# A fixed order on VectorE at the end of each recurrent step: r·h of the third batch's halves placed ahead of the first pair's last update and turns

## The chip, the cores and the metric

The kernel runs on one core of a Trainium2 chip. Its engines, with the names that the profile uses, are TensorE (PE, with PEld for the loading of its weights), VectorE (DVE), ScalarE (ACT), GpSimd (POOL) and SyncE (SP), whose queue issues nearly all of the transfers. The metric is the device time of one execution in microseconds; lower is better.

## The reference, cut to what matters

Two layers over 16 graphs of 1024 nodes with 128 features each, all with one 1024×1024 matrix `adj`. Layer 0 is one graph convolution; layer 1 is a gated recurrent cell, run five times, that aggregates over the graph in every step. Both end in a residual sum and a layernorm.

```python
support = einsum('bnf,fo->bno', x, weight)                       # layer 0
x = layernorm(x + einsum('nm,bmo->bno', adj, support) + bias)

def step(h):                                                     # layer 1, five times
    m  = einsum('nm,bmd->bnd', adj, h)                           # m_in and m_out: the same matrix
    av = concatenate([m, m], axis=-1)
    u3 = h @ u3_w.T + u3_b
    z  = sigmoid(av @ w3_w.T + w3_b + u3)
    r  = sigmoid(av @ w4_w.T + w4_b + u3)
    hv = tanh(av @ w5_w.T + w5_b + (r * h @ u5_w.T + u5_b))
    return (1 - z) * h + z * hv
x = layernorm(x + h_after_five_steps)
```

All is float32. One step for a graph is thus: aggregate, two gates z and r, the product r·h, the candidate hv, and the update h + z·(hv − h).

## The kernel before

The 16 graphs are worked in four quads of four; a graph of a quad is called a batch here and has a number k from 0 to 3. Layer 0 runs over the quads once. Layer 1 is `for q in range(NQ): for s in range(STEPS)`, 20 steps, and the change lies in this loop. A step's tensors for a quad stay on the chip: `rows` holds h with the nodes on the partitions, for the aggregation; `hid` holds h with the features on the partitions, for the gates and the update; `agg` holds the aggregated rows.

**A step has three parts.** First `aggregate` multiplies by `adj` with a seven-product scheme for 2×2 blocks, used on two levels. The outer level's seven products come as four chains, named by their numbers 12, 3, 67 and 54. Each chain (function `chain`, matmuls on L427) makes seven inner products in the order 1, 5, 6, 2, 7, 3, 4, of 1.73 us each where two outer products are made side by side. Inner product 1 of chain 12 reads `rows` of batch 0. Products 5, 6, 7 and 4 read sums that VectorE makes in `inner_sums` (L346 to L349, here called S1 to S4): S1 is a difference of batch 1 and batch 0, S2 is made from S1, and products 5 and 6 wait for them.

Secondly, `gates_of_pair` makes the gates of batches 0 and 1 together, again by seven products (L666, L685 to L691), and `reset_products` (L715) finishes the candidate's matmuls. `update` then does each half of each batch: a tanh on ScalarE (L723) and three instructions on VectorE, subtract (L724), multiply (L725), add into `hid` (L726), each working on the result of the one before. `turn_rows` (L737) transposes a whole batch of `hid` into the buffer `ypad`, and its two transfers (L748, 256 KB each) write it to the DRAM buffer `turned`; `fetch_rows` (L757, four transfers of 128 KB for a batch) reads `turned` back into `rows`, for the next step. Each of the two turns writes a part of both batches' buffers, so the fetch of batch 0 needs both turns. The last step of a quad (`last`) does otherwise: it turns to `closing` and reads the next quad's state into `hid`, while the next quad's rows come by `load_pairs` and `load` (L810, L113) right after the aggregation.

Thirdly come batches 2 and 3, in half batches called units 4 to 7. For each unit there are `gate_first` (L540, u3 product, and its copy L548), `gate_r` (L558, sigmoid L561, then r·h on VectorE, L568), `gate_z` (L573, L576), `update_products` (L581 with w5, then L582 with u5, which needs r·h), and in `update_half` a tanh (L592) and again three instructions on VectorE (L597, L598, L599). Behind unit 5 batch 2 is turned, and behind each of units 6 and 7 half of batch 3, with their fetches. S1 to S4 of the next step are made between the updates of units 6 and 7:

```python
        if urgent and h == 1:
            next_sums[0] = first_sums(rows)
            pinned(next(next_sums[0]))
```

**What sets the order.** TensorE's matmuls here, the transfers, and some instructions of VectorE are given to `tc.keep_in_program_order` (`in_order`, and `put` where it is passed); such instructions of an engine keep the order in which they are written. The rest may be moved by the framework's scheduler when the program is built; semaphores keep the data right in any case. `pin` pins only while `strict` is set, which here it is not. In a step that isn't the last of its quad, VectorE's built order from the first update is, with T for a turn of a batch, ru for r·h of unit u, and s, m, a for the three instructions of an update (the digits after them: batch, half for the first pair; unit for the rest):

```
s(0,0) m s(1,0) a m s(0,1) a m s(1,1) a m  T0  a  r4  T1  s4 m4 r5 a4 s5 m5 r6 a5  T2  r7  S1  s6 m6 a6 T3a S2 s7 m7 a7 T3b S3 S4
```

In the last step of a quad the next quad's sums (S1 to S4 of rows 0 and 1, and four smaller ones of rows 2 and 3) aren't pinned, and the scheduler has put them among the instructions of the gates of the first pair and ahead of the first update: one ahead of L657, two between it and L688, five after it.

ScalarE's and TensorE's order around this: L540 of units 4 and 5, L558 and L573 of unit 4, L540 of unit 6, L581 and L582 of unit 4, L558, L573 of unit 5, L540 of unit 7, L581, L582 of unit 5, L558 and L573 of unit 6, of unit 7, L581 and L582 of unit 6, of unit 7, then inner product 1 of the next step. In the last step of a quad the four matmuls of inner product 1 stand between L581 and L582 of unit 4.

## Time and profile before

| what | value |
|---|---|
| time, median of 3 runs | 1887.28 us (1886.15 to 1887.92) |
| the profiled execution's own time | 1888.17 us |
| its span, first to last instruction | 1886.0 us |
| TensorE busy | 1816.3 us, 96% of the span, 7092 matmuls |
| VectorE busy | 1404.3 us, 74% |
| ScalarE busy | 804.9 us, 43% |
| transfers | 161.42 MB, 86 GB/s over the span; 405328 of 421306 packets under 512 B |
| granted TensorE clock, mean | 0.980 |

In this profile a busy share is no distance from a limit: TensorE is busy for 96%, and that includes stretches at half clock. What a stage waits for is read from the table of waits (engine, line, and the engine and line that released it: total us, times, longest us), from the timeline (start, duration, engine, line, tile written and tiles read, count, and in brackets the idle time before the first of them and its releaser), and from the table of stretches (busy time of each engine in a stretch, then the granted TensorE clock, the transfer engines' busy share and GB/s). The profiled execution's own time is 2.2 us above its span and 0.9 us above the median of the runs.

### The profile page before, as it was taken

The page shows a single profiled execution, that of the slowest core. Times are in us where ns is not written, and L with a number is a line of the kernel's source. Part 1 is how long each engine was busy: PE and PEld are TensorE (multiplying, and loading weights), DVE is VectorE, ACT ScalarE, POOL GpSimd, SP SyncE. Part 2 cuts the span into 40 slices and gives each one's busy share as a digit, 9 for nine tenths or more (in the row PEclk, how much of TensorE's full clock was granted, in tenths as well). Part 3 has the DMA queues.
Part 4 walks back from the last instruction along what each step waited for, and adds up shares of the span by engine and source line. Part 5 has one row for each costly group of instructions (what it writes and reads, how often), then busy time and mean ns, then how long its engine had stood idle before and what let it go on. Part 6 is the DMA issues. An engine that isn't in the chain of part 4 may idle for free.

```text
span 1886.0 us, 21009 instructions
## 1 busy us (share of the span) xinstructions
PE 1816.3 (96%) x7092; PEld 1280.5 (68%) x7092; DVE 1404.3 (74%) x2492; ACT 804.9 (43%) x1464; POOL 102.0 (5%) x152
## 2 busy tenths in 40 slices
PE   8999999999999999999999999999999999999998
PEld 7888876674857667585765748576674757667484
DVE  6977777776686857777777767777776577777668
ACT  3355554434242443435343442534444352543436
POOL 1202210000000000000000000000000000000004
PEclk9999999999999999999999999999999999999999
DMA  8144354052242406244251423324153241505232
GB/s 259 46 134 135 112 135 103 9 112 45 68 86 71 101 12 134 45 101 86 60 123 45 112 54 92 84 62 112 37 121 80 65 82 31 123 1 123 45 90 89
DMA packets 421306, 161.42 MB, mean 86 GB/s; under 512 B 405328, under 2 KB 406480, under 8 KB 421200
## 3 DMA queue, kind: packets, MB, share of 16 engines
q1 hardware_dynamic: 418928, 153.01, 33.3%
q0 software_dynamic: 1696, 5.24, 1.0%
q10 hardware_dynamic: 576, 1.84, 0.3%
q8 instruction: 57, 0.93, 0.2%
q14 instruction: 49, 0.40, 0.1%
HBM read 93.98 MB, written 65.01 MB: 84 GB/s over the span
## 4 chain that ended last, share of the span: by engine, by line
PE 83%; DVE 10%; ACT 3%; DMA 2%; issue 2%; POOL 0%; SPq 0%; DVEq 0%; POOLq 0%; ACTq 0%
PE pb L427 23%; PE pa L427 12%; PE pc L427 12%; PE ph L582 4%; PE pu L558 4%; PE seeded L573 3%; PE ph L581 3%; PE pb L666 3%; PE pa_x L427 2%; PE pc_x L427 2%; DVE tsum L725 2%; DVE tsum L724 2%; DVE hid L726 2%; PE seeded L651 2%; PE pc L651 2%; PE seeded L666 2%
## 5 line engine op out<-in xcount | busy, mean ns | idle before, releaser
L427 PE MATMUL pb<-a,inner 128*128 128x256 f32 x760 | 187.4, 379 | 0.0
L427 PE MATMUL pb<-e,inner 128*128 128x256 f32 x672 | 162.0, 381 | 5.9 <-ACT pb L411 3.8
L427 PEld LDWEIGHTS pb<-a,inner 128*128 128x128 f32 x760 | 147.2, 194 | 16.8
L427 PE MATMUL pb<-s,inner 128*128 128x256 f32 x576 | 149.4, 382 | 1.0 <-DVE agg L415 0.8
L427 PEld LDWEIGHTS pb<-e,inner 128*128 128x128 f32 x672 | 130.7, 195 | 21.9 <-ACT pb L411 4.2
L485 DVE TENSOR_TENSOR agg<-rows 128x512 f32<-128x512 f32 x88 | 58.4, 686 | 114.7 <-ACT rows L417 114.7
L427 PE MATMUL pc<-e,inner 128*128 128x256 f32 x560 | 133.9, 379 | 0.0
L582 PE MATMUL ph<-tsum,u_t 128*128 128x512 f32 x168 | 95.9, 655 | 34.1 <-DVE tsum L568 34.1
L427 PEld LDWEIGHTS pb<-s,inner 128*128 128x128 f32 x576 | 111.0, 195 | 25.0 <-issue 9.5
L417 ACT COPY rows<-pb 128x512 f32<-128x512 f32 x44 | 25.7, 585 | 239.1 <-PE pb L427 239.1
L427 PEld LDWEIGHTS pc<-e,inner 128*128 128x128 f32 x560 | 109.2, 195 | 12.8 <-issue 1.4
L592 ACT ACTIVATE tsum<-ph,bh 128x512 f32<-128x512 f32 x82 | 56.3, 687 | 127.5 <-PE ph L582 127.4
L597 DVE TENSOR_TENSOR tsum<-tsum,hid 128x512 f32<-128x512 f32 x82 | 56.5, 689 | 66.2 <-ACT tsum L592 65.2
L298 POOL TENSOR_SCALAR rstd<-mv 128x8 f32<-128x8 f32 (+1 forms) x32 | 9.8, 305 | 1748.2 <-DVE mv L287 1716.9
L558 PE MATMUL pu<-agg,w_t 128*128 128x512 f32 x168 | 99.3, 676 | 0.1
L666 PE MATMUL pb<-first,split 64*128 64x512 f32 x228 | 85.4, 649 | 13.9 <-DVE tsum L688 13.9
L737 DVE STREAM_TRANSPOSE ypad<-hid 128x1024 f32<-128x1024 f32 (+1 forms) x92 | 97.3, 1057 | 1.7
L573 PE MATMUL seeded<-agg,w_t 128*128 128x512 f32 x168 | 89.2, 613 | 0.0
L581 PE MATMUL ph<-agg,w_t 128*128 128x512 f32 x168 | 85.8, 592 | 0.0
L582 PEld LDWEIGHTS ph<-tsum,u_t 128*128 128x128 f32 x168 | 30.9, 194 | 79.3 <-DVE tsum L568 54.9
L427 PE MATMUL pa<-s,tsum 128*128 128x256 f32 x320 | 84.7, 379 | 0.0
L540 PE MATMUL pu<-hid,u_t 128*128 128x512 f32 x168 | 82.2, 593 | 0.0
(243 smaller groups left out, 3755.2 us busy)
## 6 DMA issues: line engine op xcount, KB each, us to landing
rows<-turned SPq DMA_DIRECT2D x192, 128.0 KB, 3.1
turned<-ypad SPq DMA_DIRECT2D x92, 256.0 KB, 3.6
hvs<-saved SPq DMA_DIRECT2D x24, 512.0 KB, 4.0
turned<-ypad SPq DMA_DIRECT2D x18, 512.0 KB, 3.8
hid<-hidden SPq DMA_DIRECT2D x64, 128.0 KB, 3.3
rows<-turned SPq DMA_DIRECT2D x128, 64.0 KB, 2.2
rows<-saved SPq DMA_DIRECT2D x12, 512.0 KB, 3.6
hidden<-ypad SPq DMA_DIRECT2D x12, 512.0 KB, 4.1
```

Of the source, the lines that this page charges most:

```text
L427: product = nc.tensor.matmul(bank_of[a][:, ts(o, QT)], chunk(a, o, c), left[n][a][:, c, :], start=(a in (1, 5) and o == 0 and c == 0), sto ...
L485: nc.vector.tensor_add(agg[:, dst, HALF:], a[:, cols], b[:, cols])
L540: in_order(nc.tensor.matmul(pu, w_t["u3"], hid[:, k, ts(h, HALF)], start=True, stop=True, skip_group_check=True))
L558: in_order(nc.tensor.matmul(pu, w_t["w4"], agg[:, k, cols], start=False, stop=True, skip_group_check=True))
L573: in_order(nc.tensor.matmul(pz, w_t["w3"], agg[:, k, cols], start=False, stop=True, skip_group_check=True))
L581: in_order(nc.tensor.matmul(ph, w_t["w5"], agg[:, k, cols], start=True, stop=False))
L582: in_order(nc.tensor.matmul(ph, w_t["u5"], rh_of[k % 2][:, cols], start=False, stop=True))
L592: pin(nc.scalar.activation(hv, ph, AF.Tanh, bias=bh))
L597: pinned(nc.vector.tensor_sub(hv, hv, hid[:, k, cols]))
L651: in_order(nc.tensor.matmul(t, w_t["u3"], h, start=True, stop=True, skip_group_check=True))
L666: in_order(nc.tensor.matmul(held[p, role][e], gate_left[a][at], right[a][at], start=False, stop=True, skip_group_check=True,))
L737: op = nc.vector.transpose(t.rearrange("p (to n j c) -> p n to c j", to=4, n=n, c=2), hid[:, k, cols].rearrange("p (n to i c) -> p n to c ...
```

## The change

It has four parts, all in layer 1's loop but for one.

1. `update` is split: `candidate` does `reset_products` and the two tanh of a half, and `update` keeps the three VectorE instructions, which are now pinned. Both candidates are issued, then three of the four updates.
2. `gate_r` is called without its r·h for units 4 and 5, and `gate_rh` is called with `in_order`, so that r·h of unit 4 is pinned ahead of the fourth update of the first pair and of both turns, and r·h of unit 5 behind the turns and ahead of the update of unit 4. The turns are pinned in the steps that aren't a quad's last. `update_half` returns its VectorE part as a function, `update_rest`, which is called after r·h of unit 5 for unit 4 and at once for the other units.
3. In a quad's last step the next quad's sums are issued at unit 5 and not at unit 4, and are pinned.
4. In layer 0, at its first quad, `settle_left_12` and `load_layer1_weights` are issued as hooks ahead of inner product 4 of chain 54 and no longer at the end of chain 67. In the built program the order on ScalarE, SyncE and GpSimd is the same there as before.

The built order on VectorE in a step that isn't a quad's last is now:

```
s(0,0) m a  s(1,0) m a  s(0,1) m a  r4  s(1,1) m a  T0 T1 r5  s4 m4 a4 s5 r6 m5 a5 r7  T2  S1  s6 m6 a6 T3a S2 s7 m7 a7 T3b S3 S4
```

(In the very first step s4 and m4 stand ahead of r5.) TensorE's, ScalarE's and SyncE's orders in those steps are as before. In a quad's last step it is, with S for the sums of rows 0 and 1, S' for the smaller ones, and O for the outer sums of the next aggregation:

```
s(0,0) m a  s(1,0) m a  s(0,1) m a  r4  s(1,1) T0 m s4 a m4 T1 r5 a4  S1 S2 S3 S4 S1' s5 S2' S3' S4' m5 r6 a5 r7 T2 s6 O m6 s7 a6 m7 O a7 O O
```

and on TensorE three of the four matmuls of inner product 1 stand ahead of L582 of unit 5, and the fourth, with one of product 5, ahead of L582 of unit 6.

```diff
-    def gate_rh(u):
+    def gate_rh(u, put=None):
         k, h = UNITS[u]
         rh, cols = rh_of[k % 2], ts(h, HALF)
-        pin(nc.vector.tensor_mul(rh[:, cols], rh[:, cols], hid[:, k, cols]))
+        (put or pin)(nc.vector.tensor_mul(rh[:, cols], rh[:, cols], hid[:, k, cols]))
...
         pin(nc.scalar.activation(hv, ph, AF.Tanh, bias=bh))
+        return lambda: update_rest(k, h, urgent)
+
+    def update_rest(k, h, urgent):
+        cols = ts(h, HALF)
+        hv = rh_of[k % 2][:, cols]
         pinned = in_order if urgent else pin
...
-    def update(p, j, e, put=lambda op: op):
+    def candidate(p, j):
+        reset_products(p, j)
+        for e in range(2):
+            nc.scalar.activation(
+                rh_of[e][:, side(p, j)], held[p, f"ph{j}"][e], AF.Tanh, bias=bh
+            )
+
+    def update(p, j, e):
         cols, k = side(p, j), 2 * p + e
         hv = rh_of[e][:, cols]
-        nc.scalar.activation(hv, held[p, f"ph{j}"][e], AF.Tanh, bias=bh)
-        put(nc.vector.tensor_sub(hv, hv, hid[:, k, cols]))
-        put(nc.vector.tensor_mul(hv, hv, z_to[p][e][:, cols]))
-        put(nc.vector.tensor_add(hid[:, k, cols], hid[:, k, cols], hv))
+        in_order(nc.vector.tensor_sub(hv, hv, hid[:, k, cols]))
+        in_order(nc.vector.tensor_mul(hv, hv, z_to[p][e][:, cols]))
+        in_order(nc.vector.tensor_add(hid[:, k, cols], hid[:, k, cols], hv))
...
             gates_of_pair(tag, 0)
-            for j in range(2):
-                reset_products(0, j)
-                for e in range(2):
-                    update(0, j, e)
-            for k in range(2):
-                if last:
-                    turn_rows(k, None, closing[k])
-                    fetch_hidden(k)
-                else:
-                    turn_rows(k, None, None, not final)
-            if not last:
-                for k in range(2):
-                    fetch_rows(k)
+            candidate(0, 0)
+            candidate(0, 1)
+            update(0, 0, 0)
+            update(0, 0, 1)
+            update(0, 1, 0)
...
-                if last and u == 4:
-                    sums_of(rows, (1, 2))
-                    sums_of(rows, (3,))
-                update_half(tag, k, h, part, not last and k == 3)
+                if last and u == 5:
+                    sums_of(rows, (1, 2), True)
+                    sums_of(rows, (3,), True)
+                rest = update_half(tag, k, h, part, not last and k == 3)
+                if u == 4:
+                    return rest
+                rest()
...
             gate_first(tag, 4, "c")
             gate_first(tag, 5, 2)
-            gate_r(4)
+            gate_r(4, False)
+            gate_rh(4, in_order)
             gate_z(4)
+            update(0, 1, 1)
+            for k in range(2):
+                if last:
+                    turn_rows(k, None, closing[k])
+                    fetch_hidden(k)
+                else:
+                    in_order(turn_rows(k, None, None, not final))
+            if not last:
+                for k in range(2):
+                    fetch_rows(k)
             gate_first(tag, 6, 0)
-            step_update(4, 1)
-            gate_r(5)
+            rest = step_update(4, 1)
+            gate_r(5, False)
+            gate_rh(5, in_order)
+            rest()
             gate_z(5)
```

## The prediction, made before the changed kernel was run

> **What bounds the kernel now.** I read the page first (busy shares, costliest groups), then the waits, then one step's timeline, then the granted clock in short stretches. TensorE bounds it, and three rows say where it stands still:

> ```profile
> PE 1816.3 (96%) x7092; PEld 1280.5 (68%) x7092; DVE 1404.3 (74%) x2492; ACT 804.9 (43%) x1464; POOL 102.0 (5%) x152
> ```

> ```profile
> PE ph L582 <- DVE tsum L568: 34.1, 16, 2.1
> PE pb L666 <- DVE tsum L688: 13.9, 5, 4.2
> ...
> PE pb L427 <- DVE inner L347: 0.8, 1, 0.8
> ```

> 16 steps (all but each quad's last) lose 2.13 us each waiting for r·h of unit 4; three last steps lose about 4 us each ahead of L666. VectorE's own waits show two limits beneath:

> ```profile
> DVE inner L346 <- DMA rows<-saved: 5.3, 2, 2.8
> DVE inner L346 <- DMA rows<-turned: 4.5, 3, 1.6
> ```

> The first belongs to the last steps: a sum that waits for the next quad's rows holds up the gates behind it. The second is three ordinary steps in which S1 already waits for the turned rows to come back; this row decides my forecast. An ordinary step:

> ```profile
> 862.42 0.69 DVE L724 TENSOR_TENSOR tsum<-tsum,hid 128x512 f32<-128x512 f32 x1 [1.79 <-ACT tsum L723]
> 863.14 0.69 DVE L725 TENSOR_TENSOR tsum<-tsum 128x512 f32<-128x512 f32 x1
> 863.75 0.68 DVE L724 TENSOR_TENSOR tsum<-tsum,hid 128x512 f32<-128x512 f32 x1
> ...
> 869.17 1.24 DVE L737 STREAM_TRANSPOSE ypad<-hid 128x1024 f32<-128x1024 f32 x1
> 870.33 0.65 DVE L726 TENSOR_TENSOR hid<-hid,tsum 128x512 f32<-128x512 f32 x1
> 870.43 3.92 SPq L748 DMA_DIRECT2D turned<-ypad  x4
> 870.90 0.68 DVE L568 TENSOR_TENSOR tsum<-tsum,hid 128x512 f32<-128x512 f32 x1
> 871.50 1.24 DVE L737 STREAM_TRANSPOSE ypad<-hid 128x1024 f32<-128x1024 f32 x1
> ...
> 871.64 1.78 PE L582 MATMUL ph<-tsum,u_t 128*128 128x512 f32 x2 [2.13 <-DVE tsum L568]
> ```

> An instruction that needs the one before starts 0.72 us after it, an independent one 0.60. And stretches of 5 us from the end of this wait, in two steps:

> ```profile
> 541.02:546.02 5.00, 5.00 (x12) 2.37 (x13) 3.69 (x5) 2.63 (x4) 0.00 (x0) 1.00 0.94 199
> 871.64:876.64 5.00, 5.00 (x8) 2.21 (x9) 3.24 (x5) 1.80 (x3) 0.00 (x0) 0.66 0.94 200
> ```

> Two things: the gap of 2.13 us is followed by about 3.4 us at half clock in 13 of the 16 steps (clock 0.66 here), and not in three, as at 541; and the transfer engines are at 94% behind the turns. Steps are 82.02 us apart where the clock fell and 81.19 where it did not (708.42 to 789.61), only 0.83 less although half clock cost TensorE 1.97 us (L582 to the next step's product 1 takes 13.98 us against 14 x 0.86 = 12.01). The difference went into these waits:

> ```profile
> 545.90 4.03 SPq L757 DMA_DIRECT2D rows<-turned  x8
> 553.28 0.69 DVE L346 TENSOR_TENSOR inner<-rows 128x512 f32<-128x512 f32 x1 [1.61 <-DMA rows<-turned]
> 557.55 1.97 PE L427 MATMUL pb<-e,inner 128*128 128x256 f32 x8 [0.80 <-DVE inner L347]
> ```

> **The change part by part: ordinary steps.** Times from the first update's start (862.42 = 0).

> *r·h of unit 4.* Before: 8.48 (870.90). Now nine update instructions stand ahead of it, a triple costing 0.72 + 0.72 + 0.60 = 2.04: 3 x 2.04 = 6.12, done at 6.8 (its sigmoid ends at 5.24). TensorE is through L581 at 6.93 (869.35). The wait of 2.13 us goes, and with it the half clock. Without anything else that is 2.13 + 1.97 = 4.1 us in 13 steps.

> *r·h of unit 5.* It follows r4, the fourth triple and both turns: 6.12 + 0.60 + 2.04 + 1.16 + 1.16 = 11.08, done 11.8; TensorE wants it at 6.93 + 5 x 0.86 = 11.2. New wait 0.6. Those of units 6 and 7 come at about 14.3 and 16.2, in time. TensorE is at the next step's product 1 at 19.55, where it was at 23.2.

> *The turns.* T0 starts at 6.12 + 0.60 + 2.04 = 8.76 where it started at 6.75: 2.01 later. T1 starts at 9.92 where it was 9.08: 0.84 later. Behind them on SP stand four writes, 1 MB, and eight fetches, 1 MB. The engines are full from 871.7 to 876.9, at about 200 GB/s (last three columns: clock, share, GB/s):

> ```profile
> 873.00:874.00 1.00, 1.00 (x2) 0.34 (x1) 0.00 (x0) 0.55 (x1) 0.00 (x0) 0.50 1.02 219
> 874.00:875.00 1.00, 1.00 (x3) 0.42 (x2) 0.79 (x2) 0.14 (x1) 0.00 (x0) 0.50 0.97 201
> 876.00:877.00 1.00, 1.00 (x4) 0.51 (x3) 1.00 (x2) 0.69 (x1) 0.00 (x0) 1.00 0.86 191
> ```

> So T1's data queue behind T0's, and a T1 that comes sooner after T0 gains nothing. The fetch starts on SP when batch 1's first write has landed (876.50) and takes eight issues of 0.5. So the rows come later by T0's 2.0 us; the bound from below is T1's 0.84, if the writes didn't queue; from above 2.3, since T2's write now follows the last fetch at once. I take 2.0, as the bandwidth row fits.

> *What is late next.* In the undisturbed steps S1 starts, on landing, at 21.3 to 21.5 (553.28 - 531.80 = 21.48). Now 23.4. On VectorE S1 is pinned ahead of the updates of unit 6, their turn and S2; product 6 starts 4.27 after S1 (553.28 to 557.55). So product 6 comes at 27.7, where it was at 26.6 (half clock) or 25.7. TensorE, 3.7 us early, waits for rows and S2, and everything behind is as in the undisturbed steps.

> *Sum.* Step spacing 81.19 + 2.0 = 83.2: +1.18 where the clock fell, +2.0 where it did not. One of the 13, the quad's fourth step at 1779.46, has matmuls of the next gates to fill with (product 6 at 28.4): -0.7. Together 12 x 1.18 + 3 x 2.0 - 0.7 = +19.5 us.

> [...]

> **Quads' last steps.** The 4 us wait is this:

> ```profile
> 610.88 0.69 DVE L346 TENSOR_TENSOR inner<-rows 128x512 f32<-128x512 f32 x1 [2.76 <-DMA rows<-saved]
> ...
> 614.03 2.67 PE L666 MATMUL pb<-first,split 64*128 64x512 f32 x4 [4.19 <-DVE tsum L688]
> ```

> With the sums pinned behind r·h of unit 5 this piece is as in an ordinary step. From the seven L701 to unit 4's L540 it is 13.61, 13.33 and 13.36 us in the three (607.91 to 621.52 in the first) against 6.92 in an ordinary one (857.15 to 864.07): 6.7, 6.4 and 6.4 saved, half clock included. Against it: the eight sums (five at 0.6, the rest 0.4) now stand between r5 and r6, which puts r·h of unit 6 at 18.4 to 19.1 where TensorE wants it at 18.8, and r5 at 12.7 against 12.5: 0.6 us; up to 0.4 where L415 frees a bank for product 4. The rows have landed by then. Part 4 moves no instruction: nothing, bounds 0.5 either way from the 0.57 copies. Net -6.0 a step, -18 us.

> **Sum.** +19.5 - 18.0 + 1 us of half clock in the new gaps = +2.5 us on the profiled execution's 1888.17, hence 1890.7; that execution stands 0.9 above the median, so I say 1890.0, +2.7 rounded up. I call a change within 0.2% (3.8 us, about what a measurement of this kernel can tell) none: the forecast is no change or a little slower.

> **Rivals.**

> *The turned rows follow T1 (faster).* For: fetches wait for batch 1's write, which is 0.84 late only. Against: the engines at 94%. Rows at 22.3, step spacing 82.0: 12 x 0.0 + 3 x 0.84 - 1 = +1.5, less 18: 1871 to 1874. Half way between, 1880. It decides where the delay is under 1.5 us.

> *The clock falls in the new gaps (slower).* TensorE now stands before product 1 (about 1 us), before product 5 (1.6 to 2.0) and before product 6 (1.7). The half-clock stretches are 3.36 to 3.44 us long and their starts lie multiples of about 3.41 apart, so the clock is set window by window; with the windows laid so, 2.05 us of the gap at 459 fell into one and the clock halved, and 2.00 at 541 did not halve it. If rows come 0.3 later, the second gap passes 2.0 and about half or all of the 15 steps fall. Price at most (3.4 - 1.74)/2 = 0.83 a step, the rest lying in the next wait: +6 to +12, 1896 to 1902. [...]

> *The transfers are hidden after all (much faster).* 16 x 2.13 + 13 x 1.97 + 18 = 78 us. S1's three waits speak against it; only if rows landed by 19.5.

> **How the numbers follow.** The summed case 0.50, own range 1886 to 1895, of which slower 0.22, same 0.22, faster 0.06. Rows after T1 or half way 0.25, nearly all faster. Clock falls 0.23, slower. Hidden transfers 0.02. So slower 0.45, same 0.24, faster 0.31. The range goes from 1873 to 1901, leaving out the ends of both rivals.

> **What would show it.** Right: L582 no longer waits for L568 by 2.1; S1 waits for rows<-turned in all 15 or 16 ordinary steps, 2 to 4 us, and starts near 23.4; T0 near 8.8; product 6 waits for L347; L666's wait drops to about 2 us in total; steps 83 apart; clock 1.00 behind r·h. Wrong: S1 near 22.3 or below, or a clock of 0.66 around the next step's product 5.

## The result, and the profile after

| | before | after |
|---|---|---|
| median | 1887.19 us (12 runs, 1884.45 to 1888.69) | 1887.40 us (12 runs, 1886.04 to 1889.26) |
| ratio | | 1.0002, 95% interval 0.9993 to 1.0011 |
| profiled execution, own time / span | 1888.17 / 1886.0 us | 1886.47 / 1884.5 us |
| granted clock, mean | 0.980 | 0.997 |
| ordinary step (first update to first update) | 82.02 or 81.19 us | 82.9 to 83.5 us, median 83.09 |
| ordinary step's to last step's first update | 87.66, 88.02, 88.10 us | 82.94, 82.88, 82.97 us |

No change that can be measured: 1887.40 against a forecast of 1890.0 in a range of 1873 to 1901. Two large effects cancel. The page's busy line of the kernel after has less TensorE time than before, without any gain in the span to speak of:

```profile
PE 1799.6 (95%) x7092; PEld 1262.8 (67%) x7092; DVE 1411.3 (75%) x2492; ACT 804.7 (43%) x1464; POOL 102.2 (5%) x152
```

TensorE's and VectorE's waits after (engine, tile and line, then who released it: total us, times, longest):

```profile
PE pc L427 <- DVE inner L346: 19.6, 15, 1.8
PE pa L427 <- DMA rows<-turned: 13.1, 14, 1.2
PE pb L427 <- ACT hvs L304: 11.8, 8, 1.5
PE pb L427 <- DVE inner L347: 11.6, 8, 1.5
PE ph L582 <- DVE tsum L568: 6.9, 16, 1.7
```

```profile
DVE inner L346 <- DMA rows<-turned: 77.3, 23, 5.2
```

L582's 34.1 us have become 6.9, all of it at unit 5 now, and the 13.9 us ahead of the gates of the last steps have become 1.9 (the line is L671 now). In their place TensorE stands three times in nearly every ordinary step, ahead of products 1, 5 and 6 of the next aggregation (14, 15 and 16 times in 16 steps): 56.1 us together. The last row is VectorE's: S1 waits for the turned rows. The same step as in the prediction, by the timeline of the kernel after (first update at 863.20):

```profile
869.37 0.68 DVE L568 TENSOR_TENSOR tsum<-tsum,hid 128x512 f32<-128x512 f32 x1
...
872.02 2.37 DVE L748 STREAM_TRANSPOSE ypad<-hid 128x1024 f32<-128x1024 f32 x2
...
879.30 4.07 SPq L768 DMA_DIRECT2D rows<-turned  x8
...
886.39 0.69 DVE L346 TENSOR_TENSOR inner<-rows 128x512 f32<-128x512 f32 x1 [4.79 <-DMA rows<-turned]
...
887.23 1.97 PE L427 MATMUL pc<-e,inner 128*128 128x256 f32 x8 [1.38 <-DVE inner L346]
...
889.87 0.65 DVE L347 TENSOR_TENSOR inner<-rows,inner 128x512 f32<-128x512 f32 x1
...
890.67 1.97 PE L427 MATMUL pb<-e,inner 128*128 128x256 f32 x8 [1.47 <-ACT hvs L304]
```

Read it from the top, in us behind the first update: r·h of unit 4 at 6.17; T0 and T1 together from 8.82; the fetch from 16.10 (14.08 before); S1 at 23.19, for which VectorE waited 4.79 us. Product 5 starts 0.84 behind S1, product 6 4.28 behind it. The clock behind r·h, 0.66 in the stretch shown of before, is full (columns as there):

```profile
872.50:877.50 5.00, 4.65 (x12) 1.86 (x11) 4.86 (x7) 2.73 (x5) 0.00 (x0) 1.00 0.55 116
```

And a quad's last step, again from the timeline of the kernel after:

```profile
611.69 1.93 PE L706 MATMUL seeded<-agg,split 64*128 64x512 f32 x7
...
618.61 1.88 PE L540 MATMUL pu<-hid,u_t 128*128 128x512 f32 x4
```

From the seven matmuls (L701 before) to unit 4's L540 it is 6.92 us where it was 13.61, the same as in an ordinary step. Between the two profiled executions the span changes as follows: the 12 intervals between ordinary steps give +15.3 us, the three into the last steps −15.0, the three out of them +1.0, the stretch from the last step's first update to the end −1.8, and the first update comes 1.0 earlier. Together that is −1.5 us.

### The profile page after: what moved, and what is told of

The parts are those of the page before. It is cut to its first block, busy times and chain, and to the rows that moved or that the text cites. A ratio compares the mean times of both kernels' runs of the same rounds, so it can differ in the third digit from the quotient of the medians.

```text
span 1884.5 us, 21015 instructions
## 1 busy us (share of the span) xinstructions
PE 1799.6 (95%) x7092; PEld 1262.8 (67%) x7092; DVE 1411.3 (75%) x2492; ACT 804.7 (43%) x1464; POOL 102.2 (5%) x152
## 3 DMA queue, kind: packets, MB, share of 16 engines
q0 software_dynamic: 1696, 5.24, 1.0%
## 4 chain that ended last, share of the span: by engine, by line
PE 69%; DVE 16%; DMA 5%; ACT 4%; SPq 3%; issue 3%; POOL 0%; DVEq 0%; POOLq 0%; ACTq 0%
PE pb L427 22%; PE pc L427 11%; PE pa L427 10%; DVE ypad L748 3%; DVE tsum L736 3%; DMA rows<-turned 3%; PE pb L671 3%; DVE tsum L735 3%; PE pc_x L427 2%; PE pa_x L427 2%; DVE hid L737 2%; PE seeded L671 2%; SPq L768 2%; PE seeded L706 2%; PE pu L558 2%
## 5 line engine op out<-in xcount | busy, mean ns | idle before, releaser
L427 PE MATMUL pb<-e,inner 128*128 128x256 f32 x672 | 162.2, 381 | 26.9 <-ACT hvs L304 11.8
L427 PE MATMUL pb<-a,inner 128*128 128x256 f32 x760 | 187.4, 379 | 0.0
L427 PEld LDWEIGHTS pb<-e,inner 128*128 128x128 f32 x672 | 128.9, 194 | 47.3 <-ACT hvs L304 14.7
L427 PEld LDWEIGHTS pb<-a,inner 128*128 128x128 f32 x760 | 146.5, 194 | 17.5
L427 PE MATMUL pc<-e,inner 128*128 128x256 f32 x560 | 135.6, 381 | 19.6 <-DVE inner L346 19.6
L427 PE MATMUL pb<-s,inner 128*128 128x256 f32 x576 | 149.8, 383 | 1.2 <-DVE agg L415 0.8
L427 PEld LDWEIGHTS pc<-e,inner 128*128 128x128 f32 x560 | 108.0, 195 | 37.3 <-ACT pb L411 22.9
L427 PEld LDWEIGHTS pb<-s,inner 128*128 128x128 f32 x576 | 111.0, 195 | 26.1 <-issue 9.5
L582 PE MATMUL ph<-tsum,u_t 128*128 128x512 f32 x168 | 89.7, 616 | 6.9 <-DVE tsum L568 6.9
L748 DVE STREAM_TRANSPOSE ypad<-hid 128x1024 f32<-128x1024 f32 (+1 forms) x92 | 95.3, 1050 | 1.1
L427 PE MATMUL pa<-a,rows 128*128 128x256 f32 x320 | 77.4, 383 | 13.1 <-DMA rows<-turned 13.1
L558 PE MATMUL pu<-agg,w_t 128*128 128x512 f32 x168 | 88.0, 606 | 0.0
L581 PE MATMUL ph<-agg,w_t 128*128 128x512 f32 x168 | 85.8, 592 | 0.0
L427 PE MATMUL pa<-s,tsum 128*128 128x256 f32 x320 | 84.7, 379 | 0.0
L671 PE MATMUL pb<-first,split 64*128 64x512 f32 x228 | 82.6, 623 | 1.9 <-DVE tsum L693 1.9
L427 PEld LDWEIGHTS pa<-a,rows 128*128 128x128 f32 x320 | 61.2, 195 | 34.0 <-issue 21.8
L346 DVE TENSOR_TENSOR inner<-rows 128x512 f32<-128x512 f32 (+1 forms) x44 | 24.4, 554 | 77.7 <-DMA rows<-turned 77.3
```

What stands on the lines that cost most here:

```text
L427: product = nc.tensor.matmul(bank_of[a][:, ts(o, QT)], chunk(a, o, c), left[n][a][:, c, :], start=(a in (1, 5) and o == 0 and c == 0), sto ...
L558: in_order(nc.tensor.matmul(pu, w_t["w4"], agg[:, k, cols], start=False, stop=True, skip_group_check=True))
L581: in_order(nc.tensor.matmul(ph, w_t["w5"], agg[:, k, cols], start=True, stop=False))
L582: in_order(nc.tensor.matmul(ph, w_t["u5"], rh_of[k % 2][:, cols], start=False, stop=True))
L671: in_order(nc.tensor.matmul(held[p, role][e], gate_left[a][at], right[a][at], start=False, stop=True, skip_group_check=True,))
L748: op = nc.vector.transpose(t.rearrange("p (to n j c) -> p n to c j", to=4, n=n, c=2), hid[:, k, cols].rearrange("p (n to i c) -> p n to c ...
```

## The experiments

All of them, each against runs of the kernel before on the same chip. T0, T1, fetch and S1 are starts in us behind the first update, medians over the 15 ordinary steps ahead of the last one, from each profiled execution; so is the step spacing, which also takes in the three intervals into a last step.

| run | us | ratio, 95% interval | T0 | T1 | fetch | S1 | step |
|---|---|---|---|---|---|---|---|
| before | 1887 | | 6.75 | 9.08 | 14.06 | 21.48 | 82.02 |
| after | 1887.4 | 1.0002 [0.9993, 1.0011] | 8.82 | 9.98 | 16.15 | 23.18 | 83.09 |
| sums alone | 1868.1 | 0.9897 [0.9883, 0.9910] | 6.75 | 9.08 | 14.09 | 21.54 | 82.02 |
| order alone | 1908.1 | 1.0108 [1.0095, 1.0122] | 8.82 | 9.98 | 16.11 | 23.34 | 83.27 |
| r·h 5 between the turns | 1890.9 | 1.0017 [1.0008, 1.0026] | 8.82 | 10.56 | 16.13 | 23.19 | 83.09 |
| turn first | 1879.6 | 0.9960 [0.9947, 0.9974] | 6.77 | 11.03 | 15.61 | 22.85 | 82.76 |
| writes exchanged | 1882.6 | 0.9975 [0.9965, 0.9986] | 8.82 | 9.98 | 14.79 | 22.98 | 82.88 |
| interleaved | 1861.9 | 0.9863 [0.9848, 0.9877] | 6.75 | 9.81 | 14.38 | 21.63 | 81.52 |
| turn ahead of r·h 4 | 1854.1 | 0.9824 [0.9809, 0.9838] | 6.27 | 9.45 | 14.04 | 21.22 | 81.12 |
| no return | 1850.7 | 0.9806 [0.9789, 0.9822] | 8.82 | 9.98 | – | 16.94 | 80.87 |
| S2 behind S1 | 1889.3 | 1.0013 [1.0004, 1.0022] | 8.82 | 9.98 | 16.12 | 23.28 | 83.29 |
| the same on "turn ahead" | 1854.7 | 0.9830 [0.9816, 0.9843] | 6.27 | 9.45 | 14.03 | 21.05 | 81.06 |
| update 6 ahead of S1 | 1859.3 | 0.9856 [0.9843, 0.9869] | 8.82 | 9.98 | 16.14 | 23.34 | 81.53 |
| the same on "turn ahead" | 1835.4 | 0.9726 [0.9712, 0.9739] | 6.27 | 9.45 | 14.04 | 21.60 | 79.78 |

### Sums alone, order alone: the two halves of the change

Part 3 on the kernel before:

```diff
-                if last and u == 4:
-                    sums_of(rows, (1, 2))
-                    sums_of(rows, (3,))
+                if last and u == 5:
+                    sums_of(rows, (1, 2), True)
+                    sums_of(rows, (3,), True)
```

> The kernel before, with part 3 alone: in a quad's last step the next quad's sums are issued at unit 5 and pinned; the ordinary steps keep the order of before. Theory (the two halves of the change are independent, the last steps give and the ordinary ones take): the three intervals from an ordinary step's first update to the last step's fall from 87.7 to 88.1 us to about 83 (half-clock steps of before cost 82, as the wait of 2.13 us ahead stays), the ordinary steps stay at 82.0 and 81.2, 16 waits of 2.1 us at L582 stay; three times about 5 to 6.5 less: 1868 to 1873 us, ratio 0.990 to 0.9925. Rival (the sums only leave the gates free because r·h of units 4 and 5 is pinned ahead of them; without it they push r·h back): the 4 us wait turns up again at L582 of unit 5 or 6, and the time is 1882 to 1890, ratio 0.997 to 1.0015.

And the reverse of that diff on the kernel after, which leaves parts 1 and 2:

> The kernel after with the sums of a quad's last step back at unit 4 and not pinned, so parts 1 and 2 of the change alone. Theory: the ordinary steps are 83.1 us apart as in the changed kernel, 13 to 16 of them 1.1 to 2 us longer than before, and the last steps keep their wait of about 4 us ahead of L666: 1903 to 1908 us, ratio 1.008 to 1.011 to the kernel before. Rival (the fixed order by itself is worth nothing, the two effects are only an accident of the trace): 1885 to 1890, ratio 0.9985 to 1.0015.

Measured: 1868.11 us (−19.2) and 1908.13 us (+20.8). TensorE's waits in the run with the sums alone:

```profile
PE ph L582 <- DVE tsum L568: 34.9, 18, 2.1
...
PE pb L666 <- DVE tsum L688: 1.9, 2, 0.9
```

and in the run with the order alone:

```profile
PE pb L671 <- DVE tsum L693: 14.6, 5, 4.5
```

Each half takes away its own wait and leaves the other's. The pinned sums need no help from the new order, and the new order by itself costs a per cent. Not all of the 19.2 is the last steps: in the profiled execution these give −17.7 going in and +2.3 coming out; 2.5 comes from the ordinary steps, in six of which, not three, the clock stayed up this time, and 1.2 from an earlier first update.

### R·h of unit 5 between the turns; the turn first: which turn the rows follow

On the kernel after, `gate_rh(5, in_order)` moved between T0 and T1:

```diff
...
-                else:
-                    in_order(turn_rows(k, None, None, not final))
-            if not last:
-                for k in range(2):
-                    fetch_rows(k)
+            else:
+                in_order(turn_rows(0, None, None, not final))
...
             gate_rh(5, in_order)
+            if not last:
+                in_order(turn_rows(1, None, None, not final))
+                for k in range(2):
+                    fetch_rows(k)
```

> The kernel after with r·h of unit 5 between the two turns: T0 stays at 8.8 us behind the first update, T1 goes from 9.9 to about 10.5, nothing else moves. Theory (T0 and the throughput of the transfer engines set when the rows are back, T1 only queues behind): S1 stays at 23.2 give or take 0.2, steps 83.1 apart, the wait of 0.35 us at L582 of unit 5 goes; 1884 to 1889 us, ratio to before 0.9985 to 1.001. Rival (the rows follow T1): S1 at 23.8, 15 steps by 0.6, 1894 to 1898, ratio 1.0035 to 1.0055.

T1 came 0.58 later and nothing followed it: fetch at 16.13, S1 at 23.19, a median step of 83.09, as after. The rows don't follow T1 here. The landings of the writes say why: T1's first write is issued 0.33 later than in the kernel after (11.82 against 11.49) and lands at 16.05 in both (medians), 1.34 to 1.36 behind T0's second write. It queues behind T0's data, and the fetch starts when it has landed (16.13). Yet the time, 1890.9, is 2 us above what that theory said. In the profiled execution 2.9 of the 4.1 us against the profiled execution of after lie in one step (85.94 us, at 864.27), and 1.9 in the first two, where the rows landed up to a microsecond later; the first update was 0.8 earlier. The windows of that one step (granted clock third from the end):

```profile
884.80:890.30 5.50, 3.36 (x14) 2.73 (x15) 2.06 (x4) 0.57 (x1) 0.00 (x0) 0.98 0.83 152
890.30:893.70 3.40, 2.65 (x7) 1.70 (x6) 3.23 (x6) 1.36 (x3) 0.00 (x0) 0.50 0.30 66
893.70:896.80 3.10, 3.10 (x9) 2.39 (x9) 2.55 (x4) 0.57 (x2) 0.00 (x0) 0.50 1.09 234
```

Half clock for 6.5 us and a little at both ends, behind gaps of 1.55 us (product 1) and 1.93 us (product 5), 3.48 together, where the step shown of after has 0.84 and 1.38. The same profile has it once more, behind a gap of 2.08 us ahead of product 1 at 1712.42, for one stretch of 3.41 us:

```profile
1709.25:1712.66 3.41, 1.33 (x4) 0.46 (x3) 0.14 (x1) 0.78 (x2) 0.00 (x0) 1.00 1.04 217
1712.66:1716.07 3.41, 3.41 (x9) 2.45 (x9) 1.23 (x2) 0.08 (x1) 0.00 (x0) 0.50 1.05 215
```

This is the prediction's second rival, seen twice in one profile. It isn't the profiled execution alone: the mean granted clock of the eleven runs goes from 0.992 (1893.6 us, the slowest) to 0.998, that of the twelve runs of the kernel after from 0.996 to 0.998.

The opposite: T0 ahead of the fourth update, right behind r·h of unit 4.

```diff
+            if not last:
+                in_order(turn_rows(0, None, None, not final))
             update(0, 1, 1)
...
-                else:
-                    in_order(turn_rows(k, None, None, not final))
-            if not last:
+            else:
+                in_order(turn_rows(1, None, None, not final))
...
```

> The kernel after with the turn of batch 0 taken ahead of the fourth update, behind r·h of unit 4: T0 at 6.7 us as in the kernel before, T1 at about 11.0 instead of 9.9. Theory (T0's data queue ahead of T1's; once T0 is early enough, T1's own write sets the fetch): the fetch starts at 15.5 to 15.9 instead of 16.1, S1 at 22.6 to 23.0, 1878 to 1884 us, ratio 0.995 to 0.998. If T0 alone sets the rows: S1 at 21.2, 1855 to 1860, ratio 0.983 to 0.986. If T1 alone sets them: S1 at 24.3, 1900 to 1906, ratio 1.007 to 1.010.

T0 2.05 earlier, T1 1.05 later; the same places of the timeline:

```profile
877.81 4.06 SPq L768 DMA_DIRECT2D rows<-turned  x8
...
885.41 0.69 DVE L346 TENSOR_TENSOR inner<-rows 128x512 f32<-128x512 f32 x1 [3.96 <-DMA rows<-turned]
```

The first update of this step is at 862.20: the fetch starts at 15.61 as expected, and 1879.6 us lies in the theory's 1878 to 1884. Neither turn alone sets the rows. Over these runs the fetch starts at the later of T0's end + 6.05 and T1's end + 3.35.

### The writes exchanged: start of the fetch, or volume

On SP the write of batch 0's half from T1 goes ahead of the write of batch 1's half from T0; the fetch of batch 0 no longer has to wait for the latter.

```diff
...
+        def move(to, t):
+            tc.keep_in_program_order(nc.sync.dma_start(to.rearrange("g p x -> p g x"), t))
+
+        if kept is not None:
+            kept.append(moves.pop())
         for to, t in moves:
-            tc.keep_in_program_order(nc.sync.dma_start(to.rearrange("g p x -> p g x"), t))
+            move(to, t)
+        if kept is not None and k == 1:
+            for to, t in kept:
+                move(to, t)
...
```

> The kernel after with two of the four writes of the turned rows exchanged on SP: batch 0's half from T1 ahead of batch 1's half from T0. The fetch of batch 0 then waits for only 512 KB instead of 768 KB to land; the volume, 1 MB out and 1 MB back, the turns and everything else stay. In the runs so far the fetch started 6.05 behind T0's end or 3.35 behind T1's end, whichever was later, and S1 7.1 to 7.2 behind the fetch's start. Theory (T1's data queue behind T0's, and S1, which needs all the rows, follows the volume): the fetch starts at 14.6 to 15.4 instead of 16.1, product 1's rows are there sooner, but the other writes and fetches fill the same time, S1 stays within 0.4 of 23.2: 1880 to 1889 us, ratio to before 0.9965 to 1.001. Rival (the volume is no limit; S1 follows the start of the fetch, thus the landing of the writes that it waits for): S1 at 21.8 to 22.4, 0.8 to 1.4 less in each of 15 steps, 1866 to 1876, ratio 0.989 to 0.9945.

The step with its first update at 863.23:

```profile
878.00 5.32 SPq L776 DMA_DIRECT2D rows<-turned  x8
...
886.51 0.69 DVE L346 TENSOR_TENSOR inner<-rows 128x512 f32<-128x512 f32 x1 [4.87 <-DMA rows<-turned]
```

The fetch starts 1.36 us earlier in the median, S1 only 0.20, so S1 doesn't follow the start of the first read. That fits the theory of the volume, but doesn't prove it, for the later reads did not leave SP earlier either. The eight issues of this step and of the one of the kernel after (shortest, median and longest issue in ns, then the starts of the first and the last):

```profile
L776 SPq DMA_DIRECT2D rows<-turned x8: 422/488/1373, 878.0 to 882.8; - x8
L768 SPq DMA_DIRECT2D rows<-turned x8: 309/484/532, 879.3 to 882.8; - x8
```

Here one issue took 1.37 us, and the last read was issued at 882.8 in both, with S1 3.6 to 3.7 us behind it. Whether the bytes or the issuing of the reads sets the return, no run separates.

### Interleaved, and the turn ahead of r·h of unit 4: the rows sooner

The updates' instructions are interleaved, so that fewer of them wait for the one just ahead, and T0 goes ahead of the last multiply and add. `update` now takes the parts to be done, "s", "m" or "a" for subtract, multiply and add.

```diff
-            update(0, 0, 0)
-            update(0, 0, 1)
-            update(0, 1, 0)
+            update(0, 0, 0, "s", "m")
+            update(0, 0, 1, "s")
+            update(0, 0, 0, "a")
+            update(0, 0, 1, "m")
+            update(0, 1, 0, "s")
+            update(0, 0, 1, "a")
+            update(0, 1, 0, "m")
+            update(0, 1, 1, "s")
+            update(0, 1, 0, "a")
...
             gate_rh(4, in_order)
             gate_z(4)
-            update(0, 1, 1)
+            if not last:
+                in_order(turn_rows(0, None, None, not final))
+            update(0, 1, 1, "m", "a")
...
+            else:
+                in_order(turn_rows(1, None, None, not final))
...
```

> The kernel after with the instructions of neighbouring updates of the first pair interleaved, so that fewer of them wait for the one just ahead, and with T0 taken ahead of the last multiply and add: T0 at 6.7 us as in the kernel before, r·h of unit 4 still ahead of it (no wait of 2.1 us at L582), T1 at about 9.8 instead of 11.0 in the run with the turn first. From the four runs there, the fetch starts at the later of T0's end + 6.05 (before: 7.99 to 14.05; after: 10.07 to 16.1) and T1's end + 3.35 (turn first: 12.27 to 15.6), and S1 some 7.15 later. Theory: fetch at 14.0 to 14.5, S1 at 21.2 to 21.7, steps 81.2 to 81.7 apart, 1.5 to 2 less than after in 15 steps: 1859 to 1867 us, ratio to before 0.985 to 0.989. Rival (the rows' return isn't what sets the step any more; product 6 waits for the layernorm's L304 on ScalarE or for the copies): product 6 stays at 27.0 or later and the time at 1879 to 1888, ratio 0.9955 to 1.0005.

T0 at 6.75 with 11 instructions ahead of it (0.61 us each; in the kernel after 13, 0.68 each), T1 at 9.81, S1 at 21.63, step 81.52, 1861.9 us: all in the expected ranges. Then T0 goes ahead of r·h of unit 4 too (the lines with `turn_rows(0, ...)` move up by two calls):

> As the run with interleaved updates, but with T0 ahead of r·h of unit 4 as well: T0 at 6.1, r·h of unit 4 at 7.3 instead of 6.1, T1 at 9.3. TensorE then waits about 1.1 us at L582 of unit 4, under the 2 us behind which the clock fell in the kernel before. Theory: fetch at 13.4 to 13.9, S1 at 20.6 to 21.1, steps 80.6 to 81.2 apart, since the wait at L582 lies ahead of a longer wait for the rows: 1850 to 1860 us, ratio 0.980 to 0.9855, 5 to 10 less than the interleaved one. Rival (TensorE's wait at L582 costs its time, or takes the clock with it): 1.1 us or more in 15 steps against 0.6 gained, 1866 to 1880, slower than the interleaved one by 7 to 15.

The timeline of its step at 851.71:

```profile
857.97 1.25 DVE L752 STREAM_TRANSPOSE ypad<-hid 128x1024 f32<-128x1024 f32 x1
...
859.85 1.13 PE L582 MATMUL ph<-tsum,u_t 128*128 128x512 f32 x2 [1.05 <-DVE tsum L568]
...
873.28 0.69 DVE L346 TENSOR_TENSOR inner<-rows 128x512 f32<-128x512 f32 x1 [2.78 <-DMA rows<-turned]
```

TensorE waits 1.05 us for r·h again, half of the 2.13 us that the change had removed, and the time falls by a further 7.9 us to 1854.1. No price of that wait shows, as TensorE still waits 1.3 to 1.47 us ahead of product 6, for a sum made behind S1, and S1 waits for the rows; the gain is 0.4 us of S1. Fetch and S1 are 0.1 behind their expected ranges, since here T1's write takes over (its end at 10.69 + 3.35 = 14.04, the fetch at 14.04).

### No return: what is behind the rows

```diff
-            if not last:
-                for k in range(2):
-                    fetch_rows(k)
```

> The kernel after without the eight transfers that read the turned rows of batches 0 and 1 back in the steps that aren't a quad's last: this leaves the read-back out, so the rows of those two batches stay those of the quad's first step, and all else is done as before. It shows what the return of the rows costs in the changed kernel. Theory: product 1 follows the last L582 without a wait, S1 no longer waits, and a step takes what TensorE's work and its small waits make of it, 78 to 79.5 us instead of 83.1: 1815 to 1835 us, ratio 0.962 to 0.972. Rival (another wait stands right behind, the layernorm's L304 or r·h of units 5 to 7): 81 or more a step, 1855 to 1880.

1850.7 us: below the rival's range, and far above the theory's. S1 doesn't wait, but a step takes 80.87 us: TensorE waits 11.8 us for L415, 10.1 for L412 and 5.9 for L348 that it didn't wait for before. This run doesn't give a clean price: without the fetches the scheduler also put a quarter of product 1 (two of its eight matmuls in the trace) ahead of L582 of unit 5, and product 3 ahead of product 6.

### S2 behind S1, unit 6's update ahead of S1: the second limit

TensorE waits ahead of product 6 in all 16 ordinary steps of the kernel after, 1.47 us in 15 of them and 1.27 in the last. Half of these waits are put down to L304 on ScalarE, half to S2. Is ScalarE a limit? On VectorE S2 goes right behind S1:

```diff
             next_sums[0] = first_sums(rows)
-            pinned(next(next_sums[0]))
+            for _ in range(2):
+                pinned(next(next_sums[0]))
...
```

(The part left out takes S2 away from its old place.)

> The kernel after with S2 right behind S1 on VectorE, ahead of unit 6's update and its turn; nothing else moves on any engine. In the kernel after product 6 stands 1.47 us in all 16 ordinary steps; half of these waits are put down to S2 (L347), half to the closing layernorm's L304 on ScalarE. Theory (S2 is what product 6 waits for in all of them, since it starts 4.28 us behind S1 in both kinds; L304 only ends at about the same time): the wait goes in all 16, product 6 starts 2.8 us behind S1, each step is 1.2 to 1.47 shorter as unit 6's update and half turn come 0.7 later: 1863 to 1870 us, ratio to before 0.987 to 0.991. Rival (L304 really holds product 6 in the 8 steps): only the other half goes, 1875 to 1879, ratio 0.9935 to 0.9955. Second rival (the later half turn of batch 3 holds a later product, and the wait only moves): 1884 to 1889.

The wait went in all 16 and L304 disappeared from the list of waits, so L304 was not the cause; in the step shown of after it had only ended 0.08 us behind S2. But the time, 1889.3, was that of the second rival, a touch above its 1884 to 1889:

```profile
PE pb L427 <- DVE inner L348: 25.0, 16, 1.6
```

The wait had moved by two products, to product 7, which waits for S3 (L348). The same edit on the run with the turn ahead of r·h of unit 4:

> The run with T0 ahead of r·h of unit 4, with S2 right behind S1 besides. There product 6 waits 1.3 to 1.47 us in all 16 ordinary steps and S1 lands at 20.9 to 21.6. Theory (the two limits stand one behind the other, the return of the rows and then S2, and add): 1.2 to 1.47 less in each of 16 steps, 79.7 a step, 1830 to 1836 us, ratio to before 0.970 to 0.973. Rival (with both gone the next wait stands right behind, as in the run without the return, where steps took 80.9 with waits of 0.4 to 0.8 for the copies and sums of the products behind): 80.5 or more a step, 1842 to 1854, ratio 0.976 to 0.9825.

1854.7 against 1854.1: again nothing, and just above the rival's range, with 22.2 us of waits for S3. Moving one sum leaves the length of VectorE's chain from S1 to S3 as it was. It shortens if work leaves it, and VectorE stands idle for 4.8 us just ahead:

```diff
-        if urgent and h == 1:
-            next_sums[0] = first_sums(rows)
-            pinned(next(next_sums[0]))
         pinned(nc.vector.tensor_sub(hv, hv, hid[:, k, cols]))
         pinned(nc.vector.tensor_mul(hv, hv, z_of[k % 2][:, cols]))
         pinned(nc.vector.tensor_add(hid[:, k, cols], hid[:, k, cols], hv))
+        if urgent and h == 1:
+            next_sums[0] = first_sums(rows)
+            pinned(next(next_sums[0]))
```

> The kernel after with unit 6's subtract, multiply and add ahead of S1 on VectorE, where it stands idle for 4.8 us waiting for the rows; its turn and S2 follow S1. Nothing else moves on any engine. From the run with S2 right behind S1: the wait of 1.5 us only moved to product 7, which needs S3, since from S1 to S3 VectorE has 10 to 11 instructions of about 0.65 us, 7.05 us, and TensorE only 0.84 and three products of 1.73, 6.03. Theory (this chain behind S1 is the second limit): unit 6's three instructions run from about 19.5 to 21.6 behind the first update, S1 stays at 23.2, the waits ahead of products 6 and 7 go, 1.47 less in each of 16 steps: 1860 to 1868 us, ratio to before 0.986 to 0.990. Rival (yet another wait stands behind, as for the copies L412 and L415 in the run without the return): 1875 to 1888.

The timeline of the step at 855.34:

```profile
878.76 0.69 DVE L346 TENSOR_TENSOR inner<-rows 128x512 f32<-128x512 f32 x1 [2.36 <-DMA rows<-turned]
...
881.41 1.89 PE L427 MATMUL pb<-e,inner 128*128 128x256 f32 x8
```

S1 is where it was, 23.4 behind the first update; product 6 comes 2.65 behind S1 instead of 4.28 and TensorE doesn't wait for it, nor for product 7. The time is 1859.3 us, 28.1 less than after, a touch more than the theory's 20 to 27.

> The same edit on the run with T0 ahead of r·h of unit 4. There the rows let S1 start at 20.9 to 21.6, and unit 6's add ends at about 21.6, so S1 comes 0 to 0.7 later in some steps, 0.3 in the mean. Theory (the return of the rows and the chain behind S1 are two limits, one behind the other): 1.1 to 1.47 less in each of 16 steps, 79.7 to 80 apart, 1831 to 1838 us, ratio to before 0.970 to 0.974. Rival (S1's delay and the waits of 0.4 to 0.8 for copies and sums of the run without the return eat it): 80.5 or more a step, 1842 to 1854.

The time is 1835.4 us, 2.7% below both kernels: the two limits stand one behind the other, and what is won on each adds, though not in full (−33.3 us for the rows, −28.1 for the chain, −52.0 together). S1 now waits for unit 6's add, at 21.60 in nearly all steps. The wait of 1.05 us at L582 is still there, and no run took it out of this kernel.

## Why the prediction was right, point by point

**What bounds.** This was right. The forecast rested on S1's wait for the turned rows, three waits of at most 1.6 us before, and that row became 77.3 us in 23 waits.

**R·h of unit 4.** It was predicted at 6.12 and in time; it came at 6.17, with no wait and no half clock behind it. **R·h of unit 5.** It was predicted at 11.08 with a wait of 0.6; it came at 11.11 with one of 0.35. TensorE reached it 0.25 later than I had worked out.

**The turns and rows.** T0 was predicted at 8.76 and came at 8.82. Fetch and S1 were predicted 2.0 later, S1 at 23.4; the fetch came 2.1 later and S1 1.7 to 1.9, at 23.18. The step that decided the forecast, that the rows follow T0 by 2.0 and not T1 by 0.84, is shown by r·h 5 between the turns (T1 0.58 later, its write landing at the same time, S1 unmoved). Its reason, that the transfer engines are full, is shown for the writes (0.97 to 1.00 busy from 876 to 879.3 in the step shown of after); for the reads it stays open beside the issuing on SP. It isn't a law of T0 alone: with T0 2.05 earlier and T1 1.05 later S1 gained only 0.33, T1's data being the last in.

Had each of the 13 instructions ahead of T0 cost the 0.60 us of an independent one, T0 would have come at 7.8, an estimate from the prediction's spacing. The trace has 8.82, 0.68 on each, and interleaving the same kinds of instruction, so that fewer need the one just ahead, saved 0.07 us on each.

**What is late next.** Product 6 was predicted 4.27 behind S1 and at 27.7; it came 4.28 behind S1 and at 27.47. I expected the wait to be put down to S2; half of the time another name stood there, wrongly.

**A reading that was off.** Before, product 1 started at 23.04 (885.46 in the step shown) and not at 23.2, and at 21.34 in the steps without half clock. So half clock cost TensorE 1.70 us and not 1.97, and TensorE's lead was to be 3.5 us and not 3.7. The sum doesn't use these; the rival of the hidden transfers would have had a price of 74 us instead of 78.

**The two large terms.** They were +19.5 for the order and −18 for the sums; alone they measured +20.8 and −19.2. Each is a little larger than said, the sum the same. Of the ordinary steps 12 intervals were to give +15.8 and gave +15.3. The three last steps, with their share of the order's cost, were to give 2 x 1.18 + 2.0 − 18 = −13.6, and going in and coming out they gave −15.0 + 1.0 = −14.0. The wait of 0.6 for r·h of unit 5 there didn't come; the interval out was 0.35 longer each time.

**The small terms.** The middle was 2.6 us too high, 4.2 in the profiled execution (1890.7 against 1886.47). Of these 4.2, the two large terms give 0.9. Half clock in the new gaps was to cost 1, and none came (0.997, full in all step tails). The end of the last step was to give −0.7 and gave −1.8. The first update, which I had left alone, came 1.0 earlier; but over these runs it lies anywhere between 283.96 and 286.23, in kernels that differ only behind it, so that this microsecond is luck and no effect of the change. Part 4 shows no cost beyond that spread.

**The chances.** The time lies in the summed case's own range, 1886 to 1895, near its lower end. But the outcome that came, no change, had the smallest chance of the three, 0.24, against 0.45 for slower: that two large terms nearly cancel was forecast rightly, the lean to the slower side was not borne out.

**The rivals.** That the rows follow T1 is refuted, and the time of 1871 to 1874 with it. The clock didn't fall in the new gaps of this kernel, but it did in two steps of the run with r·h 5 between the turns, in the first of which the gaps ahead of products 1 and 5 were 1.3 us longer together; as a danger it was real. That the transfers are hidden is refuted; and the price of 78 us supposed that nothing else stands behind. With the return left out altogether only 36.7 us went.

## What to carry to other kernels

A wait that an engine loses can be worth nothing where the transfers behind it are the next limit (here the order alone took L582's wait from 34.1 us to 6.9, as in the kernel after, and cost 20.8): look up which wait stands second, and what the edit does to the start of the data that feed it. Here the cheap order was the one that kept a wait of 1.05 us on TensorE and brought the turn forward. And a wait caused by a chain went here only when work left the chain: moving one sum forward moved the wait by two products (23.4 us ahead of product 6 became 25.0 ahead of product 7), while taking three instructions from behind S1 into idle time ahead of it removed 28 us.

## What the runs showed of the hardware that was not expected

**The clock.** In the run with r·h 5 between the turns it was 0.50 for 6.8 us behind a gap of 1.93 us. It stayed at 1.00 behind a gap of 2.13 us in one step of before (541.02), and behind one of 2.78 us in the run with unit 6's update ahead of S1 (step at 367.09, clock 1.00 up to 399). So in these runs the length of a gap alone doesn't decide.

**A releaser's name.** Eight waits of 1.47 us carried the name of an instruction (L304) that ended close behind the true cause (S2), 0.08 us in the step shown. The constant distance of 4.28 us from S1 in both kinds gave it away, and the run with S2 right behind S1 showed it.
